# A graph network's quantile layer on one core: the second word's stationary sides become zero beyond the next bucket, the matmul that took the counts off is left out, and the matmuls that make the words have 128 columns

## The chip, the cores and the metric

The kernel runs on one core of a Trainium2 chip. Its time is the device time of one execution in microseconds; the time before is the median of three executions. The profile is of one further execution. Engines are named as in the profile: PE is the matrix engine's matmuls, PEld its loads of the stationary side, DVE the vector engine, ACT the scalar engine, POOL the GpSimd engine, SP the engine whose queue issues the DMAs.

## The reference, cut to what matters

Sixteen graphs of N = 1024 nodes with C = 64 channels pass through four layers. The last three are dense products with the adjacency matrix and layer norms. The first layer takes the time. For each node and channel it forms a weighted sum of three linearly interpolated quantiles (each needs the values at two ranks) over the node's neighbours, after every second neighbour of a node of high degree has been dropped:

```python
adj_d = _dilate_adj(adj, mask)                 # drop neighbours by rank in the row
sv = sort(where(valid, x, big))                # per node and channel, neighbours' values
for tau, wt in zip([0.25, 0.5, 0.75], [0.25, 0.5, 0.25]):
    pos = clip(tau * (m - 1), 0)               # m: number of neighbours
    q = sv[floor(pos)] * (1 - frac) + sv[ceil(pos)] * frac
    agg = agg + wt * q
x = layernorm(x + mlp(x + agg))                # then three more layers
```

## The kernel before, in words

The kernel sorts no neighbourhood. It sorts all 1024 values of each channel once (`sort_pair`, two graphs at a time, on DVE) and finds, for each node and each of the six ranks, the value at that rank by counting neighbours with the matrix engine. The 1024 sorted places of a channel are cut into 64 **buckets** of 16. A matmul over the nodes with the dilated adjacency `vt` as its moving side gives, for a bucket and a target node, how many neighbours lie in earlier buckets (the integer part) and which of the bucket's places are taken (a sum of different powers of two, a **word**). Sixteen places do not fit one word, so there are two: ten places in the first (`x1`), six in the second (`x2`).

**The stationary sides of these matmuls** are made on the chip by `word_part`. The rank half of `sort_pair` writes, per graph, some rows of N numbers per channel to memory (`rows_in`): the bucket of each node (row 0), its power of two for the first word (row 1), for the second word (row 3), the products of these powers with the bucket (rows 2 and 4), and a row of ones. `load_rows` brings a group's rows into `prows` (32 partitions per k). A matmul `pa<-words_by,prow` with `prows` as its stationary side and the constant `words_by` as its moving side (256 columns: 128 for each word) forms a linear function of these rows for each node and bucket; two ScalarE passes, `Relu(1 - .)` at L612 out of PSUM and again at L617 in place, clamp it. Counted from a node's own bucket, the result is 0 in the buckets before it, the node's power of two in it, one minus that power in the next bucket and 1 in all later ones. `words_by` is filled at start from `words_of` (slope and level per row, L236 to L265).

**counts** (L619) runs for each of the k = 0..3 parts of a unit: eight matmuls (one per 128 nodes) into `x1`; ScalarE writes `cc = x1 + 1024` in 16 bit (L628), which rounds it to a whole number, the count; eight matmuls into `x2`; a matmul with `neg16` (a negative identity) takes `cc` off `x1`, and ScalarE writes the first word to `dw[:, 0]` (L635); a matmul with `negup` (the negative identity moved by one bucket) takes `cc` of the bucket before off `x2`, and ScalarE writes the second word to `dw[:, 1]` (L639). Each of these 18 matmuls is one step of a generator.

**The main loop** goes over 16 graphs, 8 groups of 8 channels' rows (G8) and 2 halves of the target nodes: 256 units, with six ranks each, so 1536 **slots**, 96 to a graph. A slot has, for one rank, on DVE the comparison `mt` (L654) and the product `pr` (L658); then, one slot later each, PE matmuls and ScalarE evictions in `words` (`pw`, `qq`), `ranks` (`pr_`, `nt`), `steps` (`pv`, `val`) and `sums` (`fc`). After them come twice, for the two halves of a slot, one `word_part` of the next group (in eight of twelve slots) and six steps of the next unit's `counts`. So the counts of a unit (72 steps) fill the twelve half slots of the unit before. `mt` needs all `cc` of its unit, `pr` all `dw`.

Beside this, spread over the slots of a graph (`Spread`): the sort of a later pair (DVE), the dilation of the next graph (`dilate`: DVE, ScalarE, PE transposes `pq`), the transposed adjacency (`transposed`), and the dense layers of the graph before (`layers`).

The order on PE is the order in the program: `link` ties each matmul to the one before it. The order on DVE and ScalarE is the scheduler's. PSUM banks: `ps_x` has three, shared by `pa`, `x1` and `x2`; a new tile takes the bank that was given back first.

Of the kernel before, what the change touches and what calls it, by code (L numbers as in the profile page):

```python
# [11 lines left out]
F16 = mybir.dt.float16  # L12
# [4 lines left out]
AF = mybir.ActivationFunctionType  # L17
ALU = mybir.AluOpType
AX = mybir.AxisListType

P = 128
# [5 lines left out]
TURN = 2  # L27
# [10 lines left out]
def gnn_stack(  # L38
# [34 lines left out]
    wts = ctx.enter_context(tc.tile_pool(name="wts", bufs=5))  # L73
# [23 lines left out]
    V.tensor_copy(negup[:, 2:P], neg16[:, 0 : P - 2])  # L97
    V.tensor_copy(negup[:, 0:2], neg16[:, 0:2])
# [84 lines left out]
    e = column(11)  # L183
# [58 lines left out]
    for y in range(6):  # L242
        V.tensor_scalar(pw_[:, 6:7], pi, 2.0 * y, None, ALU.is_equal)
        V.tensor_scalar(
            pw_[:, y : y + 1], pi, 2.0 * y + 1.0, pw_[:, 6:7], ALU.is_equal, ALU.add
        )
    slope, level = column(27), column(28)
    for xi in range(2):
        yp = 1 + 2 * xi
        V.scalar_tensor_tensor(  # L250
            slope, pw_[:, yp : yp + 1], -2.0, pw_[:, 5:6], ALU.mult, ALU.add
        )
        V.scalar_tensor_tensor(
            level, pw_[:, yp + 1 : yp + 2], 2.0, pw_[:, yp : yp + 1], ALU.mult, ALU.add
        )
        V.tensor_tensor(level, level, pw_[:, 0:1], ALU.subtract)
        V.tensor_scalar(words_of[:, xi], iota_bb, slope, level, ALU.mult, ALU.add)
# [9 lines left out]
    prows = []  # L267
# [44 lines left out]
    nc.sync.dma_start(out=mask8, in_=maskT)  # L312


    rows_in = [dram1.tile([6, C, N], F16, name=f"rows{i}") for i in range(2 * TURN)]
    onerow = strm.tile([P, N], F32, tag="a", name="onerow").bitcast(F16)[0:C, 0:N]
    V.memset(onerow, 1.0)
    for r in rows_in:
        nc.sync.dma_start(out=r[5], in_=onerow)


    nosync = mybir.DependencyInfo(mybir.DependencyClass.NoSync, mybir.DependencyReason.DATA)
# [51 lines left out]
    def sort_pair(b, rows, found):  # L374

        v, _, _ = slot("sv")
        nc.sync.dma_start(out=v, in_=xT[b : b + TURN].rearrange("u c n -> (u c) n"))  # L380
        for (k, flip), kept in zip(steps(), swaps):
            v2, _, _ = slot("sv")
            m = sorts.tile([P, HALF], F16, tag="m", name="m", bufs=2)
            lo, hi = pairs(v, N, k, flip)
            l2, h2 = pairs(v2, N, k, flip)
            V.tensor_tensor(m.rearrange("p (b s) -> p b s", s=k), lo, hi, ALU.is_gt)  # L386
            nc.sync.dma_start(out=kept, in_=m)
            V.tensor_tensor(l2, lo, hi, ALU.min)  # L388
# [12 lines left out]
        found.append(xs)  # L401
        yield
        ii, _, _ = slot("ii")
        ii = ii.bitcast(I32)
        nc.gpsimd.iota(ii, pattern=[[1, N]], base=0, channel_multiplier=0)
        _, r, d = slot("sr")
        V.tensor_copy(r, ii)
        for (k, flip), kept in zip(reversed(list(steps())), reversed(swaps)):
            m = sorts.tile([P, HALF], F16, tag="m", name="m", bufs=2)
            nc.sync.dma_start(out=m, in_=kept)  # L410
            _, r2, d2 = slot("sr")
            d = d2[:, 0:HALF]
            dv = d.rearrange("p (b s) -> p b s", s=k)
            lo, hi = pairs(r, N, k, flip)
            l2, h2 = pairs(r2, N, k, flip)
            V.tensor_tensor(dv, hi, lo, ALU.subtract)
            V.tensor_tensor(d, d, m, ALU.mult)
            V.tensor_tensor(l2, lo, dv, ALU.add)  # L418
            V.tensor_tensor(h2, hi, dv, ALU.subtract)
            r, spare = r2, d2  # L420
            yield

        def keep(y, a):
            for u in range(TURN):
                nc.sync.dma_start(out=rows[u][y], in_=a[u * C : (u + 1) * C, :])


        _, bj, f = slot("sb")
        V.tensor_scalar(bj, r, 1.0 / F, 1536.0 - 15.0 / 32.0, ALU.mult, ALU.add)
        V.tensor_scalar(bj, bj, -1536.0, None, ALU.add)  # L430
        keep(0, bj)
        V.tensor_scalar(f, bj, -float(F), None, ALU.mult)
        V.tensor_tensor(f, f, r, ALU.add)
        yield

        for y, cond, top in ((1, ALU.is_lt, 13.0), (3, ALU.is_ge, 23.0)):
# [165 lines left out]
    def word_part(gr, xw, k, part):  # L602

        t = part * 2
        pa = bank(ps_x, "pa")
        for i in range(2):  # L610
            mm(pa[:, ts(i, 256)], prows[gr % 2][:, ts(t + i, P)], words_by[:, k], True, True)
        nc.scalar.activation(  # L612
            xw[:, t : t + 2].rearrange("p t x m -> p (t x m)"), pa, AF.Relu, bias=1.0, scale=-1.0
        )
        if part % 2:
            half = xw[:, t - 2 : t + 2].rearrange("p t x m -> p (t x m)")
            nc.scalar.activation(half, half, AF.Relu, bias=1.0, scale=-1.0)  # L617

    def counts(vt, words, h, cc, dw):  # L619

        hs = ts(h, HALF)
        for k in range(KC):
            xw = words[k]
            x1 = bank(ps_x, "x1")
            for j in range(T):
                mm(x1, xw[:, j, 0], vt[:, j, hs], j == 0, j == T - 1)
# [8 lines left out]
            nc.scalar.activation(dw[:, 0, k], x1, AF.Copy, bias=1024.0)  # L635
# [304 lines left out]
    def all_of(gen):  # L940
        for _ in gen:
            pass
# [77 lines left out]

    words = {0: {}}
    for k in range(KC):
        words[0][k] = wts.tile([P, T, 2, P], F16, tag="xw", name="xw")
        for part in range(4):
            word_part(0, words[0][k], k, part)
    load_rows(rows_of(0), 1)
# [10 lines left out]
    for y in range(n_units * S + S):  # L1037
# [48 lines left out]
        for half in range(2):  # L1086
            if running and nq < B * G8 and 1 <= p < 1 + 2 * KC:
                k, part = divmod(2 * (p - 1) + half, 4)
                if part == 0:
                    words.setdefault(nq, {})[k] = wts.tile(  # L1090
                        [P, T, 2, P], F16, tag="xw", name="xw"
                    )
# [65 lines left out]
```

## Time and profile before

| | |
|---|---|
| median of three executions | 10691.44 us (10684.37 to 10692.62) |
| profiled execution | 10708.47 us, span 10706.7 us |
| PE busy | 9632.1 us, 90% |
| DVE busy | 8314.7 us, 78% |
| ACT busy | 7257.7 us, 68% |
| PE matmuls in the trace | 81985 |

A matmul's duration in the trace reaches from its start to a modelled end, and the next one starts long before that end; what a matmul costs in a full stream is the distance from its start to the next one's start. In a row of grouped instructions the last figure is the mean of one in ns, and after the bar stands the idle time just before the group and what ended it.

### The profile page before, as it was taken

Reading aid. Unit: us, or ns where it says so; the run is one execution under the profiler, and the core shown is the slowest. Engines: PE = TensorE matmul, PEld = TensorE weight load, DVE = VectorE, ACT = ScalarE, POOL = GpSimd, SP = SyncE. Lnnn points to the kernel's source line nnn. Section 1 sums busy time; section 2 is a strip of 40 time slices with the busy share of each in tenths; the row PEclk is TensorE's granted clock in tenths of the full one; section 3 lists DMA queues with packets and bytes.
Section 4 is the critical chain, followed back from the end, with each engine's and each line's share of the span. In section 5 each row is a group of like instructions: output and inputs, shape, how many; then the busy total and the mean of one; then the engine's idle time right before and its main releaser. Section 6 shows DMA issues by size and latency. Waiting matters only on the chain.

```text
span 10706.7 us, 196202 instructions
## 1 busy us (share of the span) xinstructions
PE 9632.1 (90%) x81985; PEld 4090.1 (38%) x81985; DVE 8314.7 (78%) x9774; ACT 7257.7 (68%) x12321; POOL 237.1 (2%) x131
## 2 busy tenths in 40 slices
PE   0798989989899898999989999898999989999996
PEld 0343333434334343343434344343443434344442
DVE  9999989976997769976799768987666676766653
ACT  0677667677676776677766676666777777677772
POOL 0000000000000000000000000000000000000000
PEclk9899999999999999999999999999999999999997
DMA  3212332222321213222232212322122121211213
GB/s 90 64 49 61 93 91 72 77 66 69 92 79 58 70 64 93 83 59 66 68 89 87 74 49 74 86 78 77 50 60 67 53 70 62 75 50 50 60 60 107
DMA packets 735275, 760.63 MB, mean 71 GB/s; under 512 B 304049, under 2 KB 550321, under 8 KB 734385
## 3 DMA queue, kind: packets, MB, share of 16 engines
q1 hardware_dynamic: 734384, 748.08, 24.1%
q8 instruction: 642, 10.52, 0.4%
q14 instruction: 249, 2.03, 0.1%
HBM read 598.96 MB, written 148.90 MB: 70 GB/s over the span
## 4 chain that ended last, share of the span: by engine, by line
PE 51%; DVE 34%; issue 5%; DMA 5%; ACT 3%; POOL 1%; SPq 0%; POOLq 0%; DVEq 0%; ACTq 0%
PE x L335 22%; DVE pr L658 11%; PE pv L335 7%; PE pw L335 7%; PE pa L335 6%; DVE mt L654 6%; PE fc L335 3%; DMA da<-adj_dram 2%; DVE sv L388 2%; DVE sc L517 2%; DVE sv L389 2%; DVE sr L418 2%; DVE m L386 2%; PE pt L332 1%; ACT dw L635 1%
## 5 line engine op out<-in xcount | busy, mean ns | idle before, releaser
L335 PE MATMUL x<-vt,xw 128*128 128x512 f16 x16384 | 4049.1, 384 | 130.3 <-ACT dw L635 99.5
L658 DVE TENSOR_TENSOR pr<-mt,dw 128x4096 f16<-128x4096 f16 x1536 | 3510.8, 2286 | 187.2 <-ACT dw L639 169.9
L654 DVE TENSOR_TENSOR mt<-cc,rB 128x2048 f16<-128x2048 f16 x1536 | 1873.5, 1220 | 1347.2 <-PE pv L335 828.3
L335 PEld LDWEIGHTS <-xw 128*128 128x128 f16 x16384 | 1597.7, 99 | 1807.2 <-issue 455.6
L612 ACT ACTIVATE xw<-pa 128x512 f16<-128x512 f32 x2048 | 1227.7, 601 | 779.4 <-PE pa L335 765.1
L674 ACT ACTIVATE qq<-pw,col,icol 128x512 f16<-128x512 f32 x1536 | 1195.7, 778 | 589.8 <-PE pw L335 579.6
L335 PE MATMUL pv<-mt,txw 128*32 128x512 f16 x18432 | 1275.4, 382 | 0.2 <-ACT nt L683 0.2
L617 ACT ACTIVATE xw<-xw 128x1024 f16<-128x1024 f16 x1024 | 1083.7, 1058 | 22.6
L335 PE MATMUL pw<-pr,red 128*32 128x512 f16 x12288 | 939.1, 382 | 87.3 <-DVE pr L658 87.3
L335 PE MATMUL pa<-words_by,prow 128*128 128x256 f16 x4096 | 802.8, 279 | 182.2 <-DMA prow<-rows 115.2
L695 ACT ACTIVATE val<-pv 128x512 f32<-128x512 f32 x1536 | 922.6, 601 | 4.7 <-PE pv L335 4.2
L628 ACT ACTIVATE cc<-x 128x512 f16<-128x512 f32 x1024 | 613.2, 599 | 430.3 <-PE x L335 429.8
L635 ACT ACTIVATE dw<-x 128x512 f16<-128x512 f32 x1024 | 604.5, 590 | 359.8 <-PE x L335 354.4
L335 PE MATMUL fc<-val,fin 128*32 128x512 f32 x3072 | 799.6, 599 | 0.5 <-ACT val L695 0.5
L335 PEld LDWEIGHTS <-prow 128*128 128x128 f16 x4096 | 350.5, 99 | 900.7 <-issue 553.0
L335 PEld LDWEIGHTS <-txw 128*32 128x32 bf16 x18432 | 499.1, 98 | 509.9 <-issue 17.9
L335 PE MATMUL pw<-rB,subr 128*32 128x512 f16 x6144 | 617.3, 392 | 39.8 <-ACT qq L674 39.8
L639 ACT ACTIVATE dw<-x 128x512 f16<-128x512 f32 x1024 | 605.5, 591 | 0.0
L335 PE MATMUL pv<-nt,nbig 128*32 128x512 f16 x6144 | 603.4, 382 | 0.0
L510 ACT ACTIVATE vt<-da 128x512 f16<-128x512 f32 x256 | 161.0, 631 | 515.1 <-DMA da<-adj_dram 514.6
L744 POOL TENSOR_TENSOR rstd<-var,neghalf 128x8 f32<-128x8 f32 x112 | 227.4, 2030 | 9502.9 <-DVE var L742 8429.5
L335 PEld LDWEIGHTS <-red 128*32 128x32 f16 x12288 | 327.5, 97 | 268.6 <-issue 108.9
(3293 smaller groups left out, 9543.7 us busy)
## 6 DMA issues: line engine op xcount, KB each, us to landing
a<-adj_dram SPq DMA_DIRECT2D x384, 512.0 KB
a<-atd SPq DMA_DIRECT2D x256, 512.0 KB
da<-adj_dram SPq DMA_DIRECT2D x256, 256.0 KB
ac<-adj_dram SPq DMA_DIRECT2D x256, 256.0 KB
atd<-at SPq DMA_DIRECT2D x256, 256.0 KB
swaps<-m SPq DMA_DIRECT2D x440, 128.0 KB
m<-swaps SPq DMA_DIRECT2D x440, 128.0 KB
rB<-rd SPq DMA_DIRECT2D x96, 256.0 KB
```

Source lines behind the costliest of these rows:

```text
L335: link(nc.tensor.matmul(*args, **kw))
L386: V.tensor_tensor(m.rearrange("p (b s) -> p b s", s=k), lo, hi, ALU.is_gt)
L612: nc.scalar.activation(xw[:, t : t + 2].rearrange("p t x m -> p (t x m)"), pa, AF.Relu, bias=1.0, scale=-1.0)
L617: nc.scalar.activation(half, half, AF.Relu, bias=1.0, scale=-1.0)
L628: nc.scalar.activation(cc[:, k], x1, AF.Copy, bias=1024.0)
L635: nc.scalar.activation(dw[:, 0, k], x1, AF.Copy, bias=1024.0)
L639: nc.scalar.activation(dw[:, 1, k], x2, AF.Copy, bias=1024.0)
L654: V.tensor_tensor(mt, self.cc, r.unsqueeze(1).to_broadcast([P, KC, HALF]), ALU.is_le)
L658: V.tensor_tensor(pr, mt.rearrange("p k n -> p (k n)").unsqueeze(1).to_broadcast([P, 2, KC * HALF]), self.dw.rearrange("p a k n -> p a (k ...
L674: nc.scalar.activation(q, pw, AF.Identity, bias=qbias, scale=qscale)
L695: nc.scalar.activation(val, pv, AF.Relu)
L744: nc.gpsimd.tensor_tensor(rstd, var, neghalf, ALU.pow)
```

## The change

The second word's stationary side gets another form. Row 4 (power times bucket) is no longer made; the row of ones moves to its place. `words_of[:, 1]` becomes (bucket of the node) minus (bucket b) plus 1 minus (power), whose absolute value ScalarE takes out of PSUM; `Relu(1 - .)` then leaves the power in the node's own bucket, one minus the power in the next bucket, and zero in all others. So `x2` carries no count of all earlier buckets, and the matmul with `negup` and `negup` itself are left out; `x2` is evicted to `dw[:, 1]` right after its eight matmuls, without a bias and ahead of the `neg16` matmul. Since the two words now need different first passes, a `word_part` makes four blocks of nodes of one word (four matmuls of 128 columns) instead of two blocks of nodes of both (two of 256), and the tile is laid out word first. `counts` has 17 steps per k instead of 18, 68 per unit, spread five or six to a half slot.

```diff
-    negup = const.tile([P, P], F16, name="negup")
...
-    for xi in range(2):
-        yp = 1 + 2 * xi
...
+    V.tensor_scalar(words_of[:, 0], iota_bb, slope, level, ALU.mult, ALU.add)
+    V.tensor_scalar(slope, pw_[:, 4:5], -1.0, None, ALU.mult)
+    V.tensor_tensor(level, pw_[:, 0:1], pw_[:, 4:5], ALU.add)
+    V.tensor_tensor(level, level, pw_[:, 3:4], ALU.subtract)
+    V.tensor_scalar(words_of[:, 1], iota_bb, slope, level, ALU.mult, ALU.add)
...
-    rows_in = [dram1.tile([6, C, N], F16, name=f"rows{i}") for i in range(2 * TURN)]
+    rows_in = [dram1.tile([5, C, N], F16, name=f"rows{i}") for i in range(2 * TURN)]
...
-            V.tensor_tensor(t, e, bj, ALU.mult)
-            keep(y + 1, t)
+            if y == 1:
+                V.tensor_tensor(t, e, bj, ALU.mult)
+                keep(2, t)
...
-                out=prows[gr % 2][32 * k : 32 * k + 12],
+                out=prows[gr % 2][32 * k : 32 * k + 10],
...
-        t = part * 2
+        xi, t = part // 2, part % 2 * 4
         pa = bank(ps_x, "pa")
-        for i in range(2):
-            mm(pa[:, ts(i, 256)], prows[gr % 2][:, ts(t + i, P)], words_by[:, k], True, True)
-        nc.scalar.activation(
-            xw[:, t : t + 2].rearrange("p t x m -> p (t x m)"), pa, AF.Relu, bias=1.0, scale=-1.0
-        )
+        for i in range(4):
+            mm(
+                pa[:, ts(i, P)], prows[gr % 2][:, ts(t + i, P)],
+                words_by[:, k, xi * P : xi * P + P], True, True,
+            )
+        half = xw[:, xi, t : t + 4].rearrange("p t m -> p (t m)")
+        if xi:
+            nc.scalar.activation(half, pa, AF.Abs)
+        else:
+            nc.scalar.activation(half, pa, AF.Relu, bias=1.0, scale=-1.0)
         if part % 2:
-            half = xw[:, t - 2 : t + 2].rearrange("p t x m -> p (t x m)")
-            nc.scalar.activation(half, half, AF.Relu, bias=1.0, scale=-1.0)
+            whole = xw[:, xi].rearrange("p t m -> p (t m)")
+            nc.scalar.activation(whole, whole, AF.Relu, bias=1.0, scale=-1.0)
...
-                mm(x1, xw[:, j, 0], vt[:, j, hs], j == 0, j == T - 1)
+                mm(x1, xw[:, 0, j], vt[:, j, hs], j == 0, j == T - 1)
...
-                mm(x2, xw[:, j, 1], vt[:, j, hs], j == 0, j == T - 1)
+                mm(x2, xw[:, 1, j], vt[:, j, hs], j == 0, j == T - 1)
+                if j == T - 1:
+                    nc.scalar.activation(dw[:, 1, k], x2, AF.Copy)
                 yield
             mm(x1, neg16, cc[:, k], False, True)
             nc.scalar.activation(dw[:, 0, k], x1, AF.Copy, bias=1024.0)
-            yield
-
-            mm(x2, negup, cc[:, k], False, True)
-            nc.scalar.activation(dw[:, 1, k], x2, AF.Copy, bias=1024.0)
             yield
...
-                all_of(itertools.islice(counting, 6))
+                n = 2 * i + half
+                all_of(itertools.islice(counting, 68 * (n + 1) // 12 - 68 * n // 12))
```

More of the change, by code (lines that the diff above doesn't have):

```diff
@@ L94, in gnn_stack @@
     V.tensor_scalar(neg16, ident, -1.0, None, ALU.mult)
-    negup = const.tile([P, P], F16, name="negup")
-    V.tensor_copy(negup[:, 2:P], neg16[:, 0 : P - 2])
-    V.tensor_copy(negup[:, 0:2], neg16[:, 0:2])
     offdiag = const.tile([P, P], F16, name="offdiag")
@@ L241, in gnn_stack @@
     pw_ = const.tile([P, 8], F32, name="pw_")
-    for y in range(6):
+    for y in range(5):
         V.tensor_scalar(pw_[:, 6:7], pi, 2.0 * y, None, ALU.is_equal)
@@ L247, in gnn_stack @@
     slope, level = column(27), column(28)
-    for xi in range(2):
-        yp = 1 + 2 * xi
-        V.scalar_tensor_tensor(
-            slope, pw_[:, yp : yp + 1], -2.0, pw_[:, 5:6], ALU.mult, ALU.add
-        )
[L253 to L257, printed above, removed]
+    V.scalar_tensor_tensor(slope, pw_[:, 1:2], -2.0, pw_[:, 4:5], ALU.mult, ALU.add)
+    V.scalar_tensor_tensor(level, pw_[:, 2:3], 2.0, pw_[:, 1:2], ALU.mult, ALU.add)
+    V.tensor_tensor(level, level, pw_[:, 0:1], ALU.subtract)
+    V.tensor_scalar(words_of[:, 0], iota_bb, slope, level, ALU.mult, ALU.add)
[3 more added lines that the diff above has]
+    V.tensor_scalar(words_of[:, 1], iota_bb, slope, level, ALU.mult, ALU.add)
     for c2, mine in enumerate((PEVEN, PODD)):
@@ L318, in gnn_stack @@
     for r in rows_in:
-        nc.sync.dma_start(out=r[5], in_=onerow)
+        nc.sync.dma_start(out=r[4], in_=onerow)
     nosync = mybir.DependencyInfo(mybir.DependencyClass.NoSync, mybir.DependencyReason.DATA)
@@ L602, in word_part @@
     def word_part(gr, xw, k, part):
-        t = part * 2
+        xi, t = part // 2, part % 2 * 4
         pa = bank(ps_x, "pa")
-        for i in range(2):
-            mm(pa[:, ts(i, 256)], prows[gr % 2][:, ts(t + i, P)], words_by[:, k], True, True)
-        nc.scalar.activation(
-            xw[:, t : t + 2].rearrange("p t x m -> p (t x m)"), pa, AF.Relu, bias=1.0, scale=-1.0
-        )
+        for i in range(4):
[8 more added lines that the diff above has]
+            nc.scalar.activation(half, pa, AF.Relu, bias=1.0, scale=-1.0)
         if part % 2:
-            half = xw[:, t - 2 : t + 2].rearrange("p t x m -> p (t x m)")
-            nc.scalar.activation(half, half, AF.Relu, bias=1.0, scale=-1.0)
+            whole = xw[:, xi].rearrange("p t m -> p (t m)")
+            nc.scalar.activation(whole, whole, AF.Relu, bias=1.0, scale=-1.0)
     def counts(vt, words, h, cc, dw):
@@ L1022, in gnn_stack @@
     for k in range(KC):
-        words[0][k] = wts.tile([P, T, 2, P], F16, tag="xw", name="xw")
+        words[0][k] = wts.tile([P, 2, T, P], F16, tag="xw", name="xw")
         for part in range(4):
@@ L1090, in gnn_stack @@
                     words.setdefault(nq, {})[k] = wts.tile(
-                        [P, T, 2, P], F16, tag="xw", name="xw"
+                        [P, 2, T, P], F16, tag="xw", name="xw"
                     )
```

## The prediction

> **What bounds the kernel now.** The head of the page says which engines are full:
>
> ```profile
> span 10706.7 us, 196202 instructions
> ...
> PE 9632.1 (90%) x81985; PEld 4090.1 (38%) x81985; DVE 8314.7 (78%) x9774; ACT 7257.7 (68%) x12321; POOL 237.1 (2%) x131
> ...
> PE 51%; DVE 34%; issue 5%; DMA 5%; ACT 3%; POOL 1%; SPq 0%; POOLq 0%; DVEq 0%; ACTq 0%
> ```
>
> PE leads, but a third of the chain that ended last is DVE, so there are stages. I looked up where each slot starts (the first `pw<-rB,subr` on PE) and cut one pair of graphs, 6 and 7, at slots where DVE's load changes, then two single graphs; columns are length, then busy time and count of PE, PEld, DVE, ACT, POOL, PE clock, DMA share, GB/s:
>
> ```profile
> 4225.00:4578.00 353.00, 330.82 (x2829) 140.51 (x2828) 331.23 (x450) 255.17 (x432) 7.29 (x5) 0.98 0.25 75
> 4578.00:4762.00 184.00, 181.54 (x1622) 77.95 (x1620) 122.00 (x97) 131.42 (x220) 4.30 (x2) 1.00 0.18 57
> 4762.00:4872.00 110.00, 88.93 (x682) 36.95 (x681) 86.79 (x141) 68.39 (x128) 4.82 (x2) 0.92 0.51 114
> 4872.00:5242.00 370.00, 361.32 (x3140) 152.37 (x3139) 241.63 (x188) 276.00 (x462) 5.27 (x4) 1.00 0.18 56
> 5242.00:5399.00 157.00, 148.36 (x1316) 65.35 (x1319) 153.32 (x176) 108.88 (x182) 4.42 (x2) 0.98 0.22 72
> ...
> 367.00:940.00 573.00, 533.62 (x4794) 228.17 (x4793) 555.15 (x676) 426.98 (x721) 0.98 (x1) 0.99 0.19 51
> ...
> 8097.00:8606.00 509.00, 499.78 (x4403) 213.80 (x4402) 330.68 (x260) 381.41 (x638) 9.20 (x5) 1.00 0.16 51
> ```
>
> Three kinds of stage. **A**: PE full (98% in rows 2, 4 and the last), DVE two thirds: even graphs' slots 54 to 83, odd graphs' 0 to 59 while a sort goes on, all of 0 to 83 in graphs 11 to 14, all of graph 15. Graphs 2 to 10 hold 5 even and 4 odd ones, so 5 x 30 + 4 x 60 + 4 x 84 + 96 = 822 slots. **B**: the sort runs, DVE 94 to 98%, PE also 93 to 95% (rows 1, 5, 6): graph 0 (96), graph 1 to slot 83, even graphs' slots 0 to 53, odd ones' 60 to 83: 96 + 84 + 5 x 54 + 4 x 24 = 546. **C**: the last 12 slots of graphs 1 to 14, 168 in all: row 3 has PE at 81% and DVE at 79% in 110 us; the waits listed there are single ones of 2 to 5 us, on DMAs (`a`, `ac`), on `sk` and on `qq`, a chain of dilation and dense layers. Start (367 us) and tail (177 us) have hardly any counts.
>
> In A the list of waits has DVE waiting for PE (`mt` for `pv`: 61.5 us in row 4's stretch), PE for `dw` at L635 3.5 us in 14 waits, and once 3.2 us for `pr`. There every matmul taken off shortens the run.
>
> What a matmul costs, from the timeline of PE (start, length, then the group):
>
> ```profile
> 6003.14 0.39 PE L335 MATMUL pa<-words_by,prow 128*128 128x256 f16 x2
> 6003.37 1.46 PE L335 MATMUL x<-vt,xw 128*128 128x512 f16 x6
> ...
> 6017.91 0.38 PE L335 MATMUL x<-cc,neg 128*128 128x512 f16 x1
> 6018.12 0.38 PE L335 MATMUL x<-cc,negup 128*128 128x512 f16 x1
> 6018.34 0.38 PE L335 MATMUL pa<-words_by,prow 128*128 128x256 f16 x2
> 6018.97 1.46 PE L335 MATMUL x<-vt,xw 128*128 128x512 f16 x6 [0.25 <-ACT dw L635]
> ...
> 6022.20 0.40 PE L332 MATMUL pq<-ident,vt 128*128 128x128 f16 x4
> 6022.43 0.38 PE L335 MATMUL pa<-words_by,prow 128*128 128x256 f16 x2
> ```
>
> `neg` to `negup` to `pa`: 0.22 us each, not the 0.38 of the length. Two `pa` of 256 columns: 0.23. And the nearest row to the new `pa`: four 128-column transposes, each with its own load of 128 x 128 in 16 bit, took 0.23 as well, 57 ns each.
>
> **What the Trainium skill says.** "TensorE: Matmul & The Clock Gate", section "Back-to-back issue gap", gives N/2.4 + 2.5 ns (216 ns at 512 columns, 56 at 128) for matmuls alone, but about 81 ns for a sustained stream of 128-column matmuls with a load each, and 131 at 512. This trace agrees with the first (0.22, and 57 ns with the loads) and not with 131. The same page, "Step-by-step: what each phase is for", says that PE pulls loads ahead of running matmuls; the trace agrees: loads of 99 ns mean lie beside matmuls 57 ns apart. "ScalarE: Activation LUTs", section "What `ACT_TABLE_LOAD` costs", says one rate for all functions and 93 ns more for a pointer operand. The trace: `Abs` with a pointer bias (L532) 1151 ns, `Relu` with constants (L617) 1058, same size: 93 apart. The built program gives the new `Abs` constants only, so I take it at L612's 601 ns, and it loads no table more than before.
>
> **The change part by part**, against 10708.5 us for the profiled execution (span 10706.7 and 1.8 around it; 17 above the median of the runs, which I subtract again by predicting the same difference from 10691.4).
>
> 1. `negup` goes: 1024 matmuls x 0.216 = 221 us of PE stream, 0.144 a slot.
> 2. `pa`: 4096 matmuls of 256 columns become 8192 of 128. Per part 4 x 57 = 0.229 against 0.22: +0.009 x 2048 = 18 us, 0.012 a slot. Bounds: 56 ns (+6 ns a part, 12 us) to the page's 81 (+104 ns, 213 us). I take 57, measured. PEld gains 4096 x 99 ns = 405 us of busy time beside the matmuls.
> 3. ScalarE: as many passes of the same sizes; zero. In the built program no ScalarE instruction is added or removed; `cc`, `dw`, `xw` keep their slots.
> 4. Evictions in a new order: `dw[:,1]`, then `dw[:,0]`. In the built program 635 of 1024 first `x1` matmuls take over the bank of the `x1` before, given back at L635; after the change 635 take over the bank of `x2`, given back first now. PE has `negup` and a `pa` (0.22 + 0.22) to do meanwhile before, `neg` and a `pa` (0.22 + 0.23) after: the stall of 0.25 us stays as it is (99.5 us in the whole run). Zero, between -30 and +60.
> 5. `pr` at a unit's first slot waits for the last `dw`. That eviction starts one matmul, 0.22 us, earlier. It matters in B alone: 546 / 6 = 91 unit starts, at most 20 us; I take 5.
> 6. Sort: 8 `t = e * bj` of 0.69 us less on DVE (one per pair, L443), 16 DMAs of 128 KB less on SP's queue; `load_rows` moves 10 of 12 rows, same number of DMAs. 3 us in B, the DMAs zero: SP's queue is not waited for by sort or words in A and B.
> 7. Start-up: a dozen small instructions and four `negup`, 1 us.
>
> Net of 1 and 2: 0.132 us a slot. **A**: 822 x 0.132 = 109, all on the path. **B**: 546 x 0.132 = 72. There DVE is the other limit: in row 1 it works 331 / 54 = 6.13 us a slot, of which `mt` and `pr` are 1.22 + 2.29 and the rest, 2.62, is sort and dilation. If DVE's order stayed, little would be gained. But in the built program the scheduler spreads the sort further: from slot 62 to the next graph's 53 before, 60 to 54 after, some 90 slots for 87, so 2.62 falls by 3%, 0.09 us a slot. I take three quarters, 54. **C**: 22, half of it hidden behind that chain, 11. Sum: 109 + 54 + 11 + 5 + 3 + 1 = 183; rounded down for a possible new wait of DVE's in B, 175. 10691 - 175 = **10516**. What is late next in A is still PE.
>
> **Rivals.**
> - *DVE keeps B to itself* (the spread brings nothing, C's chain neither): 109 + 8 = 117 less, 10574. For it: DVE at 98% in row 5. Against: the built order.
> - *All is gained, and DVE's chain loosens as well*: 109 + 72 + 22 + 20 = 223 less, about 10468. A can't give more.
> - *Loads bound the 128-column matmuls* (ends on the other side): if each pair takes the load's 99 ns because loads stop overlapping, 8192 x 0.099 - 2048 x 0.22 = +360, less 221: +139 of PE stream, 0.09 a slot; on A, half of B and C: about +105, 10797. It decides from 82 ns a pair on, where 8192 x 0.082 = 450 + 221; at the page's 81 there is no change. Against it: `pq` at 57 with a load each.
> - *The change does not take the matmul off the path* because `neg` or the next `x1` now waits longer for ScalarE (step 4): 381 close cases x 0.4 us = 152 back: 10670, no change.
>
> **How the numbers follow.** A measurement of this kernel can tell about 0.2%, 21 us, from no change. Forecast and its like (10480 to 10560): 0.60. DVE keeps B: 0.18. All gained: 0.12. Bank waits eat it: 0.04, half of that no change. Loads bind: 0.04 slower, 0.02 at the break-even. So faster 0.92, same 0.04, slower 0.04. The range takes the rivals on the same side with their margins: 10450 to 10610.
>
> **What would show it.** No `negup` row; 8192 `pa` rows 128 wide with starts 56 to 60 ns apart (over 75: step 2 is wrong); in the stretches of A the slots shorter by 0.13 us with PE still 98% busy; PE's wait on the `dw` line near 100 us in all (over 200: step 4 is wrong); B shorter by 0.1 a slot with DVE at 94% or more. A time over 10640 would mean that one of these fails.

## The result, and the profile after

The changed kernel takes **10547.15 us** (median of four executions, 10538.66 to 10551.52) against 10692.03 for the kernel before: ratio 0.9865, 95% interval 0.9848 to 0.9882. It is 145 us faster where 175 were forecast, 31 us above the forecast and inside its range. The profiled execution took 10549.38 us, 159 less than the profiled one of before, which lay 16 above its own median.

The head of the page after:

```profile
span 10547.6 us, 202346 instructions
...
PE 9439.8 (89%) x85057; PEld 4072.7 (39%) x85057; DVE 8307.2 (79%) x9762; ACT 7287.5 (69%) x12321; POOL 236.2 (2%) x131
...
PE 48%; DVE 37%; issue 5%; DMA 4%; ACT 3%; POOL 2%; SPq 0%; POOLq 0%; DVEq 0%; ACTq 0%
```

PE has 3,072 matmuls more (8,192 of 128 columns for 4,096 of 256, less 1,024 of `negup`), yet 192 us less busy time. Its share of the chain has fallen from 51 to 48%, and DVE's has risen from 34 to 37%: what is left on the path is more of DVE's.

The stretches that answer to those of before, cut at the same slots (length, then busy time and count of PE, PEld, DVE, ACT, POOL, PE clock, DMA share, GB/s):

```profile
4148.00:4501.00 353.00, 324.92 (x2945) 139.86 (x2943) 334.62 (x460) 259.77 (x438) 9.47 (x5) 0.98 0.25 76
4501.00:4683.00 182.00, 178.58 (x1683) 77.75 (x1685) 125.10 (x98) 132.79 (x220) 4.30 (x2) 1.00 0.18 58
4683.00:4799.00 116.00, 89.05 (x700) 37.05 (x693) 86.05 (x138) 69.51 (x127) 5.23 (x2) 0.88 0.45 105
4799.00:5163.00 364.00, 354.08 (x3254) 151.43 (x3255) 241.11 (x193) 275.75 (x461) 4.91 (x3) 0.99 0.17 56
5163.00:5316.00 153.00, 143.99 (x1362) 64.38 (x1361) 149.31 (x168) 109.92 (x183) 3.89 (x2) 0.99 0.21 72
369.00:931.00 562.00, 524.15 (x4992) 227.97 (x4992) 545.43 (x662) 428.87 (x724) 0.98 (x1) 0.98 0.19 52
7974.00:8482.00 508.00, 494.99 (x4617) 214.80 (x4616) 339.00 (x268) 385.61 (x644) 9.21 (x5) 1.00 0.16 52
```

Rows are cut at whole microseconds; between the slot starts themselves, rows 2 and 4 (stage A, 30 and 60 slots) are 3.0 and 5.5 us shorter, where 4.0 and 7.9 were expected. Rows 5 and 6 (B) are 4.2 and 12.4 us shorter with DVE still at 97 to 98%. But row 1, also B, has not moved at all: PE's idle time there has grown from 22 to 28 us, as much as its work has shrunk. The last row, a whole graph's slots 0 to 83 in A, went from 515.5 us between slot starts (the row of before was cut 5 us late) to 508.2, 7.2 less where 84 x 0.132 = 11 were expected; the graph's first slots took the rest, as shown below. Row 3 (C) is 6.8 us longer.

Summed over all slots (from one `pw<-rB,subr` to the next, one profiled execution each), in us against the kernel before:

| kernel | median us | ratio to before [95%] | A | of it, first six slots | B | C |
|---|---|---|---|---|---|---|
| changed | 10547.15 | 0.9865 [0.9848, 0.9882] | -77 | +19 | -50 | -36 |
| e1 both orders of before | 10610.35 | 0.9933 [0.9919, 0.9948] | -89 | +5 | +8 | -20 |
| e2 before, no `negup` | 10641.70 | 0.9958 [0.9941, 0.9975] | -51 | +3 | 0 | -12 |
| e3 before, `pa` split | 10670.01 | 0.9982 [0.9975, 0.9989] | +10 | +5 | -2 | -58 |
| e4 changed, idle matmul | 10593.07 | 0.9915 [0.9901, 0.9930] | -9 | +25 | -60 | -56 |
| e5 changed, no Abs on ScalarE | 10494.28 | 0.9821 [0.9804, 0.9837] | -88 | -23 | -72 | -69 |
| e6 before, no Abs on ScalarE | 10701.19 | 1.0012 [1.0005, 1.0018] | +13 | -4 | -3 | -31 |
| e7 changed, VectorE's order of before | 10606.40 | 0.9927 [0.9912, 0.9943] | -84 | +9 | +20 | -26 |
| e8 changed, eviction behind | 10547.72 | 0.9872 [0.9857, 0.9887] | -77 | +20 | -51 | -30 |
| e9 as e5, changed kernel's order | 10599.62 | 0.9913 [0.9896, 0.9930] | -75 | +6 | -4 | -36 |
| e10 changed, Abs later | 10548.70 | 0.9867 [0.9852, 0.9881] | -78 | +19 | -46 | -45 |
| e11 changed, loads earlier | 10533.57 | 0.9855 [0.9840, 0.9869] | -81 | +17 | -93 | -13 |
| e12 as e5, loads earlier | 10548.11 | 0.9867 [0.9850, 0.9883] | -65 | -40 | -72 | -36 |

C reads shorter in every row, also in e3 and e6, which take no work off it: the profiled execution of before, 16 us above its median, seems to have lost that time in C. A and B are the columns to read; a C of some 15 to 30 us says nothing. The time ahead of the first slot is in none of the three columns. It is 368 us before and 365 to 371 in most runs, but 380 to 393 in e5, e6, e9, e11 and e12, which edit the dilation: 16 of its 128 blocks lie ahead of the first slot.

PE's matmuls in stage A after the change, from its timeline (start, length, group):

```profile
5939.01 0.40 PE L329 MATMUL pa<-words_by,prow 128*128 128x128 f16 x4
5939.24 1.24 PE L329 MATMUL x<-vt,xw 128*128 128x512 f16 x5
5940.32 0.38 PE L329 MATMUL x<-cc,neg 128*128 128x512 f16 x1
5940.53 0.39 PE L329 MATMUL pa<-words_by,prow 128*128 128x128 f16 x4
5941.17 1.24 PE L329 MATMUL x<-vt,xw 128*128 128x512 f16 x5 [0.25 <-ACT dw L634]
```

After `neg` comes `pa` at once; `negup` is gone. The four `pa` of 128 columns take 0.23 us to the next group's start, as the two of 256 did. And the stall before the next `x1` is 0.25 us as before, now for the eviction at L634, that of `x2`.

PE's waits, from the list of waits (us in total, times, longest; L335 and L329 are the line by which every matmul is made), first before:

```profile
PE x L335 <- ACT dw L635: 99.5, 364, 2.5
PE pw L335 <- DVE pr L658: 87.3, 58, 4.1
...
PE pa L335 <- ACT xw L612: 66.9, 37, 13.6
```

and after:

```profile
PE pw L329 <- DVE pr L656: 101.4, 77, 4.9
PE x L329 <- ACT dw L634: 101.0, 349, 4.8
...
PE pa L329 <- ACT xw L612: 67.8, 41, 4.0
...
PE pa L329 <- ACT xw L614: 27.8, 26, 3.6
```

The wait for `dw` is what it was. Two others have grown: the wait for a bank for `pa`, held by an older `pa` that ScalarE has not evicted, from 66.9 to 67.8 + 27.8 us, in up to 4 us at a time, and the wait for DVE's `pr`, from 87.3 to 101.4.

### The profile page after: what moved, and what is told of

It is laid out like the page before. It is cut to its first block, busy times and chain, and to the rows that moved or that the text cites. A ratio compares the mean times of both kernels' runs of the same rounds, so it can differ in the third digit from the quotient of the medians.

```text
span 10547.6 us, 202346 instructions
## 1 busy us (share of the span) xinstructions
PE 9439.8 (89%) x85057; PEld 4072.7 (39%) x85057; DVE 8307.2 (79%) x9762; ACT 7287.5 (69%) x12321; POOL 236.2 (2%) x131
## 4 chain that ended last, share of the span: by engine, by line
PE 48%; DVE 37%; issue 5%; DMA 4%; ACT 3%; POOL 2%; SPq 0%; POOLq 0%; DVEq 0%; ACTq 0%
PE x L329 20%; DVE pr L656 12%; PE pv L329 7%; PE pw L329 6%; DVE mt L652 6%; PE pa L329 6%; PE fc L329 3%; DVE sc L511 2%; DMA da<-adj_dram 2%; DVE sv L382 2%; DVE sr L412 2%; DVE sv L383 2%; POOL rstd L742 2%; DVE sr L411 1%; DVE sr L413 1%
## 5 line engine op out<-in xcount | busy, mean ns | idle before, releaser
L329 PE MATMUL x<-vt,xw 128*128 128x512 f16 x16384 | 4041.9, 384 | 134.1 <-ACT dw L634 101.0
L329 PEld LDWEIGHTS <-xw 128*128 128x128 f16 x16384 | 1527.6, 99 | 1757.5 <-issue 450.3
L329 PE MATMUL pv<-mt,txw 128*32 128x512 f16 x18432 | 1277.7, 383 | 2.5 <-ACT val L693 2.3
L329 PE MATMUL pw<-pr,red 128*32 128x512 f16 x12288 | 940.8, 383 | 102.0 <-DVE pr L656 101.4
L329 PE MATMUL pa<-words_by,prow 128*128 128x128 f16 x8192 | 811.3, 223 | 209.4 <-DMA prow<-rows 113.3
L329 PEld LDWEIGHTS <-prow 128*128 128x128 f16 x8192 | 584.0, 99 | 931.8 <-issue 589.8
L634 ACT ACTIVATE dw<-x 128x512 f16<-128x512 f32 x1024 | 605.2, 591 | 345.9 <-PE x L329 339.6
L329 PE MATMUL fc<-val,fin 128*32 128x512 f32 x3072 | 802.3, 600 | 0.5 <-ACT val L693 0.5
L329 PEld LDWEIGHTS <-txw 128*32 128x32 bf16 x18432 | 500.9, 98 | 512.9 <-issue 23.4
L329 PE MATMUL pw<-rB,subr 128*32 128x512 f16 x6144 | 618.1, 392 | 17.7 <-ACT qq L672 17.6
L329 PE MATMUL pv<-nt,nbig 128*32 128x512 f16 x6144 | 604.7, 382 | 0.0
L504 ACT ACTIVATE vt<-da 128x512 f16<-128x512 f32 x256 | 161.7, 634 | 461.9 <-DMA da<-adj_dram 461.6
L329 PEld LDWEIGHTS <-red 128*32 128x32 f16 x12288 | 327.9, 97 | 289.3 <-issue 133.7
```

Source lines behind the costliest of these rows:

```text
L329: link(nc.tensor.matmul(*args, **kw))
L634: nc.scalar.activation(dw[:, 1, k], x2, AF.Copy)
```

## Experiments

Where an order is held, every instruction of an engine is tied to the one before it by a dependency without a semaphore, so that the scheduler can't place it otherwise; the edit is in each case

```diff
+        for i, j in zip(order, order[1:]):
+            tc.add_manual_dep(mine[j], mine[i].name, info, reason="order written down")
```

with `order` read off the built program of the kernel named. Holding an order seems to cost nothing by itself: e8, which holds VectorE in its own order and whose edit changed little, takes 10547.72 us against 10547.15. For ScalarE, and for the kernel before, no run shows this alone.

### e1: is B's gain the scheduler's order?

The changed kernel, VectorE's and ScalarE's order that of the kernel before, with the two `dw` evictions in the changed kernel's sequence.

> The changed kernel with the instruction order of the kernel before on DVE and ScalarE (written down instruction by instruction; only the two dw evictions of a k stand in the changed kernel's sequence). Theory 1: the gain missing from the prediction was lost by the scheduler's new order at the starts of graphs and in the even graphs' sort stretch; with the old order back, stage A falls by 0.13 us a slot in all its 822 slots (109 us, the first six slots of a graph included, which rose by 19 us in the changed kernel), B by about 54 and C by 10 to 20: about 10510. Theory 2, as in the prediction: B gained only because the new order spreads the sort further; with the old order B gains at most 18 us: about 10550, like the changed kernel. Rival: order does not matter at all: 10547 with the same loss at graph starts.

Measured: 10610.35 us, 63 above the changed kernel and above all three forecasts. A keeps its gain (-89), B loses all of it (+8 against -50), and the first six slots of A's graphs cost only 5. So B's gain hangs on the new order, and the same new order costs some 15 us at the graphs' starts. By parts B is less simple: the odd graphs' slots 60 to 83 keep their gain with the old order (-17 us against -19), while the even graphs' slots 0 to 53 get 21 us longer than before the change, where the new order made them 5 shorter.

### e2: the matmul alone

In the kernel before (own orders held), `negup`'s matmul is left out; the second word is evicted with a scale to keep it in 16 bit, which changes what the kernel computes.

```diff
-            mm(x2, negup, cc[:, k], False, True)
-            nc.scalar.activation(dw[:, 1, k], x2, AF.Copy, bias=1024.0)
+            nc.scalar.activation(dw[:, 1, k], x2, AF.Copy, scale=2.0**-12)
```

> The kernel before without the negup matmul and nothing else (order on DVE and ScalarE that of the kernel before, written down; dw[:,1] is evicted without the subtraction and scaled down, so the second word's values are not those of the reference). Theory: the matmul's 0.216 us x 1024 goes, but in the 381 places where the next x1 waits for the bank that L635 gives back, negup covered half of that wait, so the wait there grows by 0.216 us: A falls by 118 - 44 = 74 us, B by 10 to 40, C by 5: 10570 to 10605, and PE's wait on the dw line L635 rises from 99 us to about 180. Rival: the eviction order is nothing and the matmul is everything: 10692 - 190 = about 10500, wait on L635 still 99 us.

Measured: 10641.70 us, above the range of the theory: A gains 51, which is 0.063 a slot and not 0.144, and B nothing. The list of waits tells where the rest is:

```profile
PE x L335 <- ACT dw L635: 174.2, 380, 2.8
```

75 us more than before. `negup` had been filling part of PE's wait for the bank of `x1`, which is evicted at L635 and taken over next. There are 381 places where only a `pa` stands between the last counting matmul (`neg`, `negup`) and the next `x1`. PE stalls at nearly all of them, for 0.25 us in the median before and 0.47 in e2. In the changed kernel the bank of `x2` comes free first, because its eviction stands ahead of the `neg` matmul, and the wait stays at 101 us. e1 has the same order as e2 but for that pair of evictions (and the split): its median stall is 0.25, and its undisturbed slot (one of slots 10 to 83 of graphs 11 to 14) takes 6.017 us against 6.069. So the early eviction is worth some 0.05 us a slot, and the matmul by itself 0.080 (6.149 to 6.069).

### e3: the split alone

In the kernel before (own orders held), each `pa` of 256 columns becomes two of 128.

```diff
-        for i in range(2):
-            mm(pa[:, ts(i, 256)], prows[gr % 2][:, ts(t + i, P)], words_by[:, k], True, True)
+        for i in range(4):
+            mm(
+                pa[:, ts(i, P)], prows[gr % 2][:, ts(t + i // 2, P)],
+                words_by[:, k, i % 2 * P : i % 2 * P + P], True, True,
+            )
```

> The kernel before with each 256-column pa matmul as two of 128 columns (same stationary block loaded twice, 8192 instead of 4096; order on DVE and ScalarE that of the kernel before). The prediction's step 2 alone: +0.009 us a part, 0.012 us a slot: +10 to +18 us, 10702 to 10710. Rival, loads bound pairs of 128 columns: from 81 ns a pair (+104 ns a part) +110 us, 10800, up to +200.

Measured: A +10 us, 0.012 a slot as priced, but half of it stands in the first six slots of the graphs. In the slots 10 to 83 of graphs 11 to 14, which nothing disturbs, a slot goes from 6.1495 to 6.1547 us: the split costs 0.005 there. The group's row, from the groups of instructions:

```profile
L335 PE MATMUL pa<-words_by,prow 128*128 128x128 f16 x8192 | 808.4, 222 | 143.9 <-DMA prow<-rows 113.3 <-ACT xw L615 29.9 <-issue 0.3
```

The 222 ns are a modelled length; from start to start the median is 56 ns. In the total the kernel came out 19 us faster, not 10 to 18 slower. The interval (0.9975 to 0.9989) excludes no change, so this is more than noise; it lies in C, and what makes it stays open.

### e4: give a matmul back

In the changed kernel (own orders held), a matmul with a zero stationary side stands before `neg`.

```diff
+    nc.gpsimd.memset(zero16, 0.0)
...
+            mm(x1, zero16, cc[:, k], False, False)
             mm(x1, neg16, cc[:, k], False, True)
```

> The changed kernel with one 512-column matmul more per k, whose stationary side is zero, between the last x2 matmul and neg16 (order on DVE and ScalarE that of the changed kernel; the results do not change). Theory: +0.216 us x 1024 of stream, but 0.216 us more cover for the 381 close waits on the dw eviction: A +74 us, B +30 to +50, C +5 to +15: 10655 to 10685, and PE's wait on L634's eviction falls from 101 us to about 20 to 40. Rival, stream time is all that counts: A +118, B +50, C +20: about 10735.

Measured: 10593.07 us, 46 above the changed kernel and far below the range of the theory. In A it costs 68 us (-9 against -77), close to the 74 forecast; an undisturbed slot grows by 0.083 us, not 0.144, because PE's wait shrinks. The row of the counts' matmuls, whose idle time is led by 101.0 us for `dw` in the changed kernel:

```profile
L331 PE MATMUL x<-vt,xw 128*128 128x512 f16 x16384 | 4027.5, 383 | 41.5 <-ACT dw L636 15.4 <-ACT xw L614 12.9 <-ACT xw L616 0.8
```

101.0 has become 15.4. B, forecast 30 to 50 us slower, is not slower for its share of the 1,024 matmuls (-60 against -50): with this order, PE's stream does not decide there.

### e7: which engine's order

As e1, but only VectorE's order is held.

> The changed kernel with VectorE's instructions held in the order of the kernel before, ScalarE's order free. Theory: stage B's gain of 50 us comes from VectorE's new order, which spreads the sort over three more slots; with the old one B is within 15 us of the kernel before (as it was with both engines held, +8), A keeps its -90, and the time is 10590 to 10620 us. Rival: ScalarE's order made the difference, and then B stays at -40 to -55 and the time at 10540 to 10560.

Measured: 10606.40 us, B +20. The wait that replaces B's gain, from the list of waits:

```profile
PE pw L329 <- DVE pr L656: 220.8, 92, 5.0
```

101.4 in the changed kernel. Holding VectorE's order is enough to lose B's gain; ScalarE's is not needed for it. What VectorE itself waits for, first before, then in e7:

```profile
DVE sr L417 <- DMA m<-swaps: 6.0, 3, 4.9
```

```profile
DVE sr L411 <- DMA m<-swaps: 31.5, 19, 3.3
```

The sort exchanges values through memory (`swaps`). With less to do on PE, the old order brings VectorE to the next step of the sort before the exchange has landed (31.6 us in all in e1, 4.2 in the changed kernel). In B's slots in all, VectorE is idle 155 us before, 187 in e7, 183 in e1 and 135 in the changed kernel: an order laid out for another program's times is not neutral.

### e8: the eviction's place

In the changed kernel (VectorE's order held), the eviction of `x2` is written behind that of `x1`.

```diff
-                if j == T - 1:
-                    nc.scalar.activation(dw[:, 1, k], x2, AF.Copy)
                 yield
             mm(x1, neg16, cc[:, k], False, True)
             nc.scalar.activation(dw[:, 0, k], x1, AF.Copy, bias=1024.0)
+            nc.scalar.activation(dw[:, 1, k], x2, AF.Copy)
```

> The changed kernel with the eviction of the second words' counts put back behind that of the first difference, as the kernel before has it, with VectorE's order held as in the changed kernel. Theory: PE's next word of counts takes the bank of the second words, which now comes free one ScalarE pass (0.4 to 0.6 us) later, and nothing runs in between since the count matmul is gone: PE's wait on that line rises from 101 us to 200 to 300, stage A is 40 to 90 us longer than in the changed kernel, and the time is 10600 to 10660 us. Rival (the prediction's step that set the eviction's place at nothing): under 15 us, 10540 to 10565.

Measured: no difference, 10547.72 us, and PE waits 85.2 + 17.7 us for the two evictions. But in the trace ScalarE, whose order was free, still takes `x2` first in 623 of the 1,024 cases, and in 366 of the 381 places where a late bank would stall PE. In the other 15 PE stalls seven times, 0.46 us in the median, as in e2. The run can't tell what the place is worth in all; e1 beside e2 does.

### e5, e6: the graphs' first slots

After the change the first ten slots of graphs 3, 5, 7, 9 and 11 to 14 take 69 us longer, all eight together, than those of graph 15, beside which no next graph is dilated. Before, it was 45. In the first six of these slots PE stood 35.6 us before, 17.8 of them for `pr` and 7.9 for the bank of `pa`; after, 50.7 us, 4.9 for `pr` and 43.5 for the bank of `pa`. ScalarE's timeline at the start of graph 11, changed kernel:

```profile
7365.21 1.06 ACT L617 ACTIVATE xw<-xw 128x1024 f16<-128x1024 f16 x1
7368.68 1.15 ACT L526 ACTIVATE vt<-sc,sk 128x1024 f16<-128x1024 f16 x1 [2.41 <-DVE sk L523]
7369.73 0.76 ACT L672 ACTIVATE qq<-pw,col,icol 128x512 f16<-128x512 f32 x1
7370.40 0.68 ACT L681 ACTIVATE nt<-pr__90848,col 128x512 f16<-128x512 f32 x1
7370.97 0.59 ACT L693 ACTIVATE val<-pv 128x512 f32<-128x512 f32 x1
7371.44 0.60 ACT L612 ACTIVATE xw<-pa 128x512 f16<-128x512 f32 x1
```

and PE's at the same time:

```profile
7367.50 1.46 PE L329 MATMUL x<-vt,xw 128*128 128x512 f16 x6
7372.10 0.58 PE L329 MATMUL pa<-words_by,prow 128*128 128x128 f16 x4 [3.14 <-ACT xw L612]
```

VectorE, just before:

```profile
7365.91 2.29 DVE L656 TENSOR_TENSOR pr<-mt,dw 128x4096 f16<-128x4096 f16 x1
...
7368.49 0.15 DVE L523 TENSOR_SCALAR sk<-sk 128x1 f32<-128x1 f32 x1
```

The dilation's Abs (L526) stands 2.41 us for `sk`, which DVE makes between its long passes; behind it in ScalarE's order wait `qq`, `nt`, `val` and the eviction of `pa`, and PE stands 3.14 us. The edit takes Abs off ScalarE; VectorE compares twice instead, with the factors of `sk` changed to fit.

```diff
...
-            nc.scalar.activation(q, cum, AF.Abs, bias=sk[:, 3:4])
             yield
-            V.tensor_scalar(q, q, sk[:, 4:5], 0.25, ALU.is_equal, ALU.max)
+            V.tensor_scalar(q, cum, sk[:, 3:4], 0.25, ALU.is_equal, ALU.max)
+            V.scalar_tensor_tensor(q, cum, sk[:, 4:5], q, ALU.is_equal, ALU.max)
```

> The changed kernel, with the dilation's Abs pass over `cum` taken off ScalarE: VectorE compares `cum` with both values itself (one more VectorE pass per half, the result is the same). Theory: the 19.5 us that stage A lost in its graphs' first six slots come from ScalarE standing at that Abs, which waits for VectorE's `sk`, with the eviction of `pa` queued behind it. Then the loss goes (first six slots of A 15 to 27 us shorter than in the changed kernel), C gets a little shorter too, and the 128 extra VectorE passes at about 0.69 us cost stage B up to 25 us: 10505 to 10545 us against the changed kernel's 10547. Rival: the loss comes from VectorE's new order itself; then the first six slots stay, B pays its 25 us, and the time is about 10570.

> The same edit of the dilation in the kernel before the change. Theory: there the order left PE no long wait for `pa` at graph starts, so the edit saves stage A less than 8 us, while the extra VectorE passes cost B up to 25 us: 10680 to 10715 us against 10692. Rival: ScalarE's Abs holds PE up at graph starts in either kernel; then this one falls by 20 us or more, as much as the changed one.

Measured: in the changed kernel 10494.28 us, 53 less, below the forecast range and **the fastest of all versions**; in the kernel before 10701.19, 0.12% more, while its first slot starts 16 us later. The first six slots of A fall by 42 us in the first, by 4 in the second. So far the theory. But 31 us come back in A's other slots (slot 6 of such a graph takes 9 to 11 us where it took 6.03), B falls by 21 where it was to pay, C falls by 33, and the first slot starts 13 us later. The graphs' first slots alone do not explain 53 us, so the order was tested apart.

### e9: the same edit, no new order

e5's kernel, with VectorE and ScalarE held in the changed kernel's order.

> The changed kernel with the dilation's Abs pass done on VectorE, as in the earlier run, but with VectorE's and ScalarE's instructions held in the changed kernel's own order: ScalarE's 128 Abs passes drop out of it, and VectorE's two comparisons stand where its one stood. Theory: ScalarE's stand at Abs is itself what holds `pa` up, so the gain stays without any new order: first six slots of A 30 to 45 us shorter than in the changed kernel, in all 10490 to 10520 us. Rival: the earlier run gained by the order that the scheduler found for the edited program; then the first six slots fall by less than 15 us, and the extra VectorE passes (0.49 and 1.28 us in place of 0.48) leave 10540 to 10580 us.

Measured: 10599.62 us, 52 *above* the changed kernel and above the rival's range too. The theory falls as an account of e5. PE's waits for `pa` did go (67.8 + 27.8 to 2.5 + 6.5 us), but another took their place. ScalarE at the start of graph 11:

```profile
7434.81 0.60 ACT L614 ACTIVATE xw<-pa 128x512 f16<-128x512 f32 x1
7439.45 0.63 ACT L504 ACTIVATE vt<-da 128x512 f16<-128x512 f32 x1 [4.05 <-DMA da<-adj_dram]
...
7442.59 0.77 ACT L672 ACTIVATE qq<-pw,col,icol 128x512 f16<-128x512 f32 x1
```

and PE:

```profile
7443.42 1.92 PE L329 MATMUL p<-wv,fin 96*32 96x512 f32 x4 [4.21 <-ACT qq L672]
```

ScalarE, no longer held at Abs, comes to the next block's copy (L504) before its load has landed, stands there 4.05 us, and `qq` waits behind it. The excess of the first ten slots is 59 us instead of 69; B loses 46 in an order made for the shorter compare: VectorE works 35 us longer in its slots (0.49 + 1.28 us for 0.48) and is idle 11 longer. e5's gain is thus that of the order which the scheduler found for the edited program.

### e10: Abs a sub-step later

```diff
-            yield
             m = cum[:, N - 1 : N]
...
+            yield
             nc.scalar.activation(q, cum, AF.Abs, bias=sk[:, 3:4])
             yield
```

> The changed kernel with one `yield` of the dilation moved: it stands between the computing of `sk` and the Abs pass instead of between the scan and `sk`, so Abs is issued a sub-step later, when `sk` should be done. No instruction is added or taken away. Theory: it is the wait for `sk`, not the 1.15 us of the pass, that holds the eviction of `pa` up; ScalarE's idle time before the Abs line falls from 236 us to under 80, the first six slots of A lose 20 to 40 us, VectorE pays nothing, and the time is 10490 to 10525 us. Rival: VectorE then waits for the Abs instead, or ScalarE's own 1.15 us is what matters, and the time stays at 10535 to 10565 us.

Measured: 10548.70 us. ScalarE's idle time before Abs is 238 us (236 in the changed kernel): in the trace, at the start of graph 11, the last `sk` passes stand behind the same `pr` and just ahead of Abs again, so the wait was not moved. A miss that tells nothing on the theory.

### e11, e12: the loads of the adjacency blocks

VectorE reads ScalarE's copy and not the block, in the changed kernel (e11) and in e5's (e12); the block's buffers come free earlier.

```diff
-                V.tensor_scalar(nb[:, ts(h, HALF)], a[h], 0.0, None, ALU.is_gt)
...
+            V.tensor_scalar(nb, q, 0.0, None, ALU.is_gt)
```

> The changed kernel, in which VectorE takes `nb` from ScalarE's half-precision copy of the adjacency block and not from the block itself (one pass of 1,024 columns in place of two of 512): the block's buffers come free as soon as ScalarE has read them, so the next load starts earlier. The Abs pass on ScalarE stays. Theory (Abs waiting for `sk` sets the graph starts): the first six slots of A stay within 12 us of the changed kernel's, VectorE's saving (two passes of 0.42 us against one of about 0.48, 128 times, so 46 us, of which a third to a half lies in B) gives B 10 to 25 us, and the time is 10515 to 10545 us. Rival (ScalarE's stand before `vt<-da` holds the evictions up just as much, 462 us of idle time in all): the first six slots fall by over 20 us and the time to 10480 to 10510 us.

> The same edit of the adjacency block together with the Abs pass done on VectorE (scheduler's own order), so that ScalarE has neither of the dilation's waits as long as before. Theory: ScalarE's idle time before `vt<-da` falls from the 604 us of the version without Abs to under 500, stage B gains 10 to 25 us by VectorE's shorter work, and the time is 10450 to 10485 us, the fastest of all versions, against 10494 for the one without Abs alone. Rival: VectorE's compare now stands waiting for ScalarE's copies with the product passes queued behind it, and the time is 10495 to 10550 us.

Measured, e11: 10533.57 us, in the range of its theory: the first six slots stay (+17 against +19). But the loads are not cleared by this. ScalarE's idle time before the copies fell from 462 to 285 us, and that before Abs rose from 236 to 412: some 697 us in all as before the edit, so the wait only moved on to Abs. B falls by 42 us more than the changed kernel's, above the 10 to 25 expected; C takes 23 back and the later first slot 11. e12: 10548.11 us, slower than e5; its theory was wrong, though ScalarE's idle time before the copies did fall, from 604 to 363 us. The first six slots are now almost free of excess (9.5 us in eight graphs against 69), but slot 6 takes 13 to 14.5 us. VectorE there, in graph 11:

```profile
7404.99 2.28 DVE L511 TENSOR_TENSOR_SCAN sc<-sc 128x1024 f16<-128x1024 f16 x1
7407.20 1.20 DVE L652 TENSOR_TENSOR mt<-cc,rB 128x2048 f16<-128x2048 f16 x1
...
7409.07 0.49 DVE L527 TENSOR_SCALAR vt<-sc,sk 128x1024 f16<-128x1024 f16 x1
7409.59 1.28 DVE L528 SCALAR_TENSOR_TENSOR vt<-sc,sk,vt 128x1024 f16<-128x1024 f16 x1
7410.80 2.28 DVE L656 TENSOR_TENSOR pr<-mt,dw 128x4096 f16<-128x4096 f16 x1
```

and PE:

```profile
7407.28 0.40 PE L329 MATMUL pw<-rB,subr 128*32 128x512 f16 x4
7413.13 1.04 PE L329 MATMUL pw<-pr,red 128*32 128x512 f16 x8 [5.45 <-DVE pr L656]
```

Scan, seven small passes and the compare stand ahead of `pr`, and PE waits 5.45 us for it. The rival had the time right, but not the way: VectorE never waited for ScalarE's copies (0.0 us of idle time before it reads them), it had too much to do ahead of `pr`. The excess of the first ten slots is 72 us, where it began (69).

## Why the prediction was right

**The net of steps 1 and 2 held within 0.002 us a slot where nothing disturbs them.** In slots 10 to 83 of graphs 11 to 14 a slot went from 6.149 to 6.015 us, 0.134 less; the net of the two steps was 0.132. The split alone measured 0.005 there (e3), less than the 0.012 taken. The loads' rival is out: the 8,192 `pa` start 56 ns apart in the median, while their loads, 99 ns in mean, lie beside them. The price of about 81 ns in the Trainium skill ("TensorE: Matmul & The Clock Gate", "Back-to-back issue gap") is not seen here. Two figures beside this step do not come out, and nothing rests on them: four times 56 ns is 4 ns a part above 0.22 us, 8 us in all and not 12; and PEld's busy time did not grow by 405 us but went from 4090.1 to 4072.7.

**Step 4 (bank waits at zero) held**: 101.0 us against 99.5. e2 shows why it was not idle to ask: without the eviction moved ahead, 0.064 of the matmul's 0.144 us a slot come back as a wait. The rival that priced this at 152 us named the right wait; the change carries the remedy in itself.

**Steps 3 and 7**: the two first passes take 599 (Relu) and 603 ns (Abs), 601 had been assumed. The first slot starts at 369.1 us against 367.9: start-up lost 1 us instead of gaining it.

**A was the mis-sized term: 109 forecast, 77 measured.** 822 x 0.134 = 110 is there in the undisturbed slots, but the excess at the starts of eight graphs grew from 45 to 69 us, 24 us. The step that failed is "all on the path", and with it "What is late next in A is still PE": in a graph's first slots the dilation, and ScalarE's evictions behind it, are late next. Of the 24 us some 15 are the new order's (with the old one the excess is 54, e1); the other 9 came with the old order too, where PE waits 24.7 us for `pr` at these starts instead of 17.8. Some 9 us more lie elsewhere, 5 of them in the even graphs' slots 54 to 83 and 3 in graph 15, and are not traced.

**B was right, and in part for the reason given: 54 forecast, 50 measured.** The order of VectorE makes it: held to the old one, B gains nothing (e1 +8, e7 +20). The spread is there: in the trace the sort's compares (`sv`, `sr`) run from an odd graph's slot 58 to the next graph's 51 before and to its 53 after, and VectorE works 31 us less in B's slots (up to 5 of them the products left out in the sort) and 38 more in A's, where it is not the limit. That is 0.057 us a slot, where 0.09 was worked out. The other 19 us are idle time that VectorE lost in B (155 to 135 us), which the prediction did not have. So the size was a lucky sum. Graphs 0 and 1 and the odd graphs gave 45 of it, the even graphs only 5, because their slots 0 to 11, in which some four of a dilation's eight blocks fall, became 9 us longer while 12 to 53 became 15 us shorter.

**C**: 11 forecast, 36 read, but C reads 31 and 58 shorter in e6 and e3 too, for a reason that is open. From the medians, 145 - 77 - 50 leaves 18. It can't be told closer. Steps 5 and 6 (5 and 3 us) are below what the runs can tell.

Open stays why the scheduler's order for e5 is better by 105 us than the changed kernel's for the same program (10494 against 10600); that its order makes the difference is shown (e9), which of its moves does is not. Open too is whether another order for the changed kernel would do as well.

## What to carry to other kernels

A matmul that runs while the bank needed next is still being evicted hides part of that eviction. Before taking it out, see which bank is taken over next and evict that one first, or part of the gain turns into a wait (here 0.064 of 0.144 us a slot). Where a scheduler lays out the engines, a change of the work is also a change of every order: price the two apart by holding the old order, since here the order was worth some 60 of 145 us. But read the result by parts, since the old order can also fit the new program worse than it fitted the old one (VectorE's 31.5 us for `swaps` in e7). And a side job that waits on ScalarE for another engine or a load makes the evictions that stand behind it late (2.41 us at Abs, 4.05 us at a copy). Taking one such wait away moved it to the next member of the chain: from the copies to Abs in e11, from Abs to the copies in e9, and on to VectorE's `pr` in e12.

## What the runs showed of the hardware

One 512-column matmul more or less in a stream that PE fills costs 0.216 us from start to start. There are two of these matmuls to three slots, so the full price is 0.144 us a slot; where the matmul lay in a bank's wait, its worth on the run was 0.08: 0.080 when taken out (e2, 6.149 to 6.069) and 0.083 when put in (e4, 6.015 to 6.098). A comparison of two tensors with a pointer operand (`scalar_tensor_tensor`, 1,024 columns of 16 bit) took 1.28 us on VectorE, 2.6 times the `tensor_scalar` of the same size (0.49).
